# Third phase of a fused attention and expert-layer kernel worked in the order of the slots, with rows gathered once and scattered to the output

## The chip, the cores and the metric

One core of a Trainium2 chip runs the whole kernel. The metric is the device time of one execution in microseconds; the time of a kernel is the median of several executions. Engines are named as in the profile: PE (TensorE, with PEld for its weight loads), DVE (VectorE), ACT (ScalarE), POOL (GpSimd), SP (SyncE, which here only issues DMAs).

## The reference

The input x has 8 x 1024 rows (L = 8, N = 1024; 8192 tokens in all) of D = 256 numbers in float32. Two blocks follow each other, each with a residual and a layer norm:

```
x = LN0(x + A(x))       # A: 16 heads of 64 channels, attention among
                        # the 64 channels' scalars of each token, causal
x = LN0(x + F(x))       # LN0: layer norm without gain and offset
F(x):
  y1 = LN(x + MHA(x); ln1_g, ln1_b)   # 4 heads of 64, attention over L = 8
  gates = softmax(y1 @ wg); idx = argmax(gates)           # 8 experts
  loc  = rank of the token among those with its idx;  keep = loc < 1024
  slot = idx * 1024 + loc                                 # where keep
  disp[slot] = y1
  h = disp[e] @ w1[e] + b1[e];  o = h @ w2[e] + b2[e]     # no nonlinearity
  m = gate * o[slot] where keep, else 0
  return LN(y1 + m; ln2_g, ln2_b)
```

So a token that is late for a full expert gets no expert output, and the slots of an expert with fewer than 1024 tokens stay empty. At the end stand two norms in a row: F's, with ln2_g and ln2_b, then the outer LN0 over x + F(x).

## The kernel before, in words

`fused_kernel` (L46) runs three phases, one after the other. Rows are handled in 64 tiles of 128 tokens (NT), token t*128 + p on partition p.

`phase_a` (L85) is the first block. Its last instruction for a tile is a product with the output weights on PE (L408); then `r` (L413), the statistics and two small POOL operations (`norm_scalars`, L63: `ve` at L70, `rs` at L72), the normed tile (L419), and a store to the DRAM tensor x1_d on SP's queue.

`phase_b` (L506) is the attention over L, with 8 groups of 128 positions n (8 tiles of 128 tokens each, one per l). Beside the attention of group j (`scores`, `weights`, `weighted`) pieces of other work are set into the order by hand in `fills(j)` (L793): the projections of group j+1, the output rows of group j-1, and a quarter each of expert j's weights. The output rows go in four pieces of two l each: `output` (L704: POOL adds the offset to x in `residual`, L699, PE multiplies, DVE adds to `r`, L717), `normal` (L720: two DVE rows, then two POOL operations with ln1_g and ln1_b, L727, and a store to y1_d on SP), `turn_y` (L730, transposition) and `logits` (L743, copied to `lg` at L755). `expert` (L765) multiplies w1 by w2 of an expert into w12, since nothing nonlinear lies between them, and collects b1*w2 + b2 in `acc` on DVE (L782); `expert_bias` (L788) sums that over partitions with a product of ones into `bias`. In every group SP also stores zeros into disp_d (L867).

`phase_c` (L891) follows in four steps, in an order written out by hand for PE, ACT, DVE and SP, while POOL is scheduled by the framework.

1. Gating over all 64 tiles at once (L940 to L954): softmax of `lg`, the largest as `gate`, the first expert that has it as `hot`. Slots: prefix products on PE (L959, L961), a scan along the tiles (L963), `loc` (L970), then `to` and `back`, the row numbers to write to and to read from (L972 to L988). Meanwhile y1 is loaded into SBUF as `ya` (L909).
2. 64 indexed DMAs (L994), issued by POOL, write the rows of `ya` to their slots in disp_d.
3. Experts: 16 loads of 512 slots (`load`, L1012), transposition (L1024), products with w12 (L1050), plus bias (L1057), store to moe_d (L1064); x1 is loaded again into `xa` (L1045) and ln2_b added (L1065).
4. Norms, 16 turns of four tiles in token order (`order`, L1169): `fetch` (64 indexed loads from moe_d on POOL, L1089), `gates` (a diagonal matrix from the gate on ACT, L1102), `mix` (PE adds moe times gate and `ya` by products, L1115 and L1118), `stats` (L1130 and L1131), `power` (POOL, L1142), `offset` (L1147), `normed` (ACT, L1154), `gain` (DVE, ln2_g, L1164), the same once more with `xa` for the second norm, and a store to `out`.

Of the kernel before, what the change touches and what calls it, by code (L numbers as in the profile page):

```python
# [39 lines left out]
CAP = L * N // E  # L41
EPS = 1e-5
# [3 lines left out]
def fused_kernel(ctx: ExitStack, tc: tile.TileContext, a: dict, out: bass.AP):  # L46
# [12 lines left out]
    y1_d = dram.tile([L * N, D], FP, name="y1_d")  # L59
    disp_d = dram.tile([2 * E * CAP, D], FP, name="disp_d")  # L60
    moe_d = dram.tile([E * CAP + 1, D], FP, name="moe_d")

# [15 lines left out]
    w12 = late.tile([P, DC, E, D], FP, name="w12")  # L78
    bias = late.tile([P, E, D], FP, name="bias")
    lg = late.tile([P, NT, E], FP, name="lg")  # L80
    phase_b(tc, a, ident, x1_d, y1_d, disp_d, w12, bias, lg, norm_scalars)
    phase_c(tc, a, ident, x1_d, y1_d, disp_d, moe_d, w12, bias, lg, norm_scalars, out)


# [421 lines left out]
def phase_b(tc, a, ident, x1_d, y1_d, disp_d, w12, bias, lg, norm_scalars):  # L506
# [8 lines left out]
    with (  # L515
# [15 lines left out]
        for n in ("in_b_v", "out_b", "ln1_g", "ln1_b"):  # L531
            rows[n] = wp.tile([P, D], FP, name=f"row_{n}")
            nc.scalar.dma_start(rows[n], a[n].partition_broadcast(P))
# [7 lines left out]
        acc = wp.tile([P, E, D], FP, name="acc")  # L541
        nc.gpsimd.memset(acc, 0.0)
        nc.sync.dma_start(acc[0:1].rearrange("p e d -> p (e d)"), a["b2"].rearrange("(o e) d -> o (e d)", o=1))
        ones = wp.tile([P, P], FP, name="ones")
        nc.gpsimd.memset(ones, 1.0)
# [10 lines left out]
        zeros = wp.tile([P, 1024], FP, name="zeros")  # L556
        nc.gpsimd.memset(zeros, 0.0)
# [3 lines left out]
        y1_v = y1_d.rearrange("(l j p) d -> j p l d", p=P, j=NJ)  # L561
# [158 lines left out]
        def normal(j, l0):  # L720
            r, sc = G["r", j, l0]
            y = kp.tile([P, 2, D], FP, name="y")
            G["y", j, l0] = y
            for l in range(2):
                nc.vector.tensor_scalar(y[:, l, :], r[:, l, :], sc[l][0], sc[l][1], ALU.subtract, ALU.mult)
            for n, op in (("ln1_g", ALU.mult), ("ln1_b", ALU.add)):
                nc.gpsimd.tensor_tensor(y, y, rows[n][:, None, :].to_broadcast([P, 2, D]), op)  # L727
            nc.sync.dma_start(y1_v[j][:, l0 : l0 + 2, :], y)
# [14 lines left out]
        def logits(j, l0):  # L743
# [11 lines left out]
            nc.vector.tensor_copy(lg.rearrange("p (l j) e -> p l j e", j=NJ)[:, l0 : l0 + 2, j, :], ps[:, : 2 * E].rearrange("p (l e) -> p l e", l=2))  # L755
# [32 lines left out]
        def expert_bias(e):  # L788
            ps = pf.tile([P, 512], FP, name="fill")
            nc.tensor.matmul(ps[:, :D], ones, acc[:, e, :], start=True, stop=True)  # L790
            nc.scalar.copy(bias[:, e, :], ps[:, :D])

        def fills(j):  # L793
# [15 lines left out]
            put(0, not N and O, expert_bias, prv)  # L809
# [3 lines left out]
            put(0, N and O, expert_bias, prv)  # L813
# [27 lines left out]
            put(3, O, logits, prv, 6)  # L841
            put(3, X, expert, j, 3)
            put(3, N, project_qk, nxt, 1, 1, 0)
            put(3, N, project_qk, nxt, 1, 1, 1)
# [3 lines left out]
        for j in range(-1, NJ + 1):  # L848
# [4 lines left out]
            for n in range(4):  # L853
# [10 lines left out]
                if live:  # L864
                    if n < 2:
                        z = (2 * j + n) * 512
                        nc.sync.dma_start(  # L867
                            disp_d[z : z + 512, :].rearrange("(p r) d -> p (r d)", p=P), zeros
                        )
# [21 lines left out]
def phase_c(tc, a, ident, x1_d, y1_d, disp_d, moe_d, w12, bias, lg, norm_scalars, out):  # L891
# [4 lines left out]
    SH = 4  # L896
    with (
        tc.tile_pool(name="cone", bufs=1) as op,
        tc.tile_pool(name="cwork", bufs=4) as kp,
        ExitStack() as stage,  # L900
        tc.manual_schedule(engines={ET.PE, ET.Activation, ET.DVE, ET.SP}),
    ):
        pp = stage.enter_context(tc.tile_pool(name="cp", bufs=3, space=PSUM))
# [31 lines left out]
        def over_experts(v):  # L935
            return v[:, :, None].to_broadcast(ALL)

# [292 lines left out]
```

## Time and profile before

| what | us |
|---|---|
| median of three runs (5261.21 to 5263.25) | 5261.26 |
| the profiled execution's own time | 5258.0 |
| its span on the core (clock granted on average 0.978) | 5256.2 |
| PE busy | 4961.1 |
| DVE / ACT / POOL busy | 3013.8 / 3359.9 / 3364.5 |
| last product of phase A ends | 4335.2 |
| last logits copied (L755) | 4888.53 |
| first / last indexed store (L994) begins | 4907.49 / 4987.44 |
| first indexed load (L1089) | 5078.03 |

The span begins with the first and ends with the last instruction of the profiled execution, 1.8 us less than that execution's time. The page gives the busy time of each engine, the same in 40 slices, the DMA queues, the chain of work that ended last, and the costliest groups of instructions. In a row of a group: line, engine, operation, names of output and inputs, shapes and how many of them; after the bar the busy time and the mean in ns of one; after the second bar the idle time of the engine ahead of them and what ended it. The timeline gives start and length of each instruction in us, and in brackets how long its engine had been idle and on what it waited.

### The profile page before, as it was taken

Reading aid. Unit: us, or ns where it says so; the run is one execution under the profiler, and the core shown is the slowest. Engines: PE = TensorE matmul, PEld = TensorE weight load, DVE = VectorE, ACT = ScalarE, POOL = GpSimd, SP = SyncE. Lnnn points to the kernel's source line nnn. Section 1 sums busy time; section 2 is a strip of 40 time slices with the busy share of each in tenths; the row PEclk is TensorE's granted clock in tenths of the full one; section 3 lists DMA queues with packets and bytes.
Section 4 is the critical chain, followed back from the end, with each engine's and each line's share of the span. In section 5 each row is a group of like instructions: output and inputs, shape, how many; then the busy total and the mean of one; then the engine's idle time right before and its main releaser. Section 6 shows DMA issues by size and latency. Waiting matters only on the chain. (4 is left out here: it accounts for less than half of the span.)

```text
span 5256.2 us, 190381 instructions
## 1 busy us (share of the span) xinstructions
PE 4961.1 (94%) x80084; PEld 3377.1 (64%) x80084; DVE 3013.8 (57%) x5908; ACT 3359.9 (64%) x4114; POOL 3364.5 (64%) x6939
## 2 busy tenths in 40 slices
PE   8999999999999999999999999999999988997177
PEld 4666666666666666666666666666666655666066
DVE  5666666566665666666666656666656643555145
ACT  5777777777777777777777777777777763443025
POOL 5766776766767677666767766676777661333625
PEclk9999999999999999999999999999999998999599
DMA  2222222222222222222222222222222212221463
GB/s 75 47 48 48 48 48 48 48 47 47 48 48 49 48 49 47 47 48 48 48 47 49 48 47 48 48 49 48 49 48 46 48 40 88 90 93 57 143 218 98
DMA packets 603408, 313.53 MB, mean 60 GB/s; under 512 B 388146, under 2 KB 562355, under 8 KB 602547
## 3 DMA queue, kind: packets, MB, share of 16 engines
q1 hardware_dynamic: 396116, 147.14, 12.3%
q0 software_dynamic: 202752, 151.40, 9.7%
q8 instruction: 626, 10.26, 0.8%
q10 hardware_dynamic: 3680, 2.83, 0.2%
q14 instruction: 234, 1.92, 0.1%
HBM read 82.76 MB, written 50.33 MB: 25 GB/s over the span
## 5 line engine op out<-in xcount | busy, mean ns | idle before, releaser
L324 ACT ACTIVATE e<-pair 128x1024 f32<-128x1024 f32 x3072 | 2977.5, 1021 | 1236.3 <-PE pair L308 1236.3
L368 POOL DMA_DIRECT2D nd<-S x4096 | 1951.1, 484 | 612.2 <-DVE S L358 419.8
L308 PE MATMUL pair<-R,L 32*128 32x128 f32 (+1 forms) x32768 | 1606.3, 322 | 3.5 <-POOL event L279 3.5
L358 DVE COPY S<-sum 128x512 f32<-128x512 f32 x1024 | 707.2, 691 | 1469.4 <-PE sum L347 1159.3
L308 PEld LDWEIGHTS pair<-R,L 32*128 32x128 f32 x32768 | 1271.9, 186 | 49.7 <-POOL event L279 4.1
L338 PE MATMUL sum<-e,V 128*32 128x256 f32 x16384 | 1285.8, 385 | 4.9 <-DVE S L358 4.9
L265 POOL DMA_DIRECT2D R<-qm x2048 | 973.4, 483 | 73.5 <-issue 40.2
L347 PE MATMUL sum<-e,V 128*32 128x128 f32 x16384 | 823.7, 273 | 0.0
L347 PEld LDWEIGHTS sum<-e,V 128*32 128x32 f32 x16384 | 533.1, 110 | 352.8 <-issue 1.8
L338 PEld LDWEIGHTS sum<-e,V 128*32 128x32 f32 x16384 | 406.5, 109 | 236.8 <-DVE qm L232 41.8
L296 PE MATMUL pair<-late,sel 32*128 32x256 bf16 (+1 forms) x6144 | 499.4, 313 | 9.6 <-ACT e L324 9.6
L219 DVE COPY V<-vT 32x128 f32<-32x128 f32 x2048 | 456.8, 223 | 28.1
L377 DVE RECIPROCAL att<-nd 128x256 f32<-128x256 f32 x256 | 447.4, 1748 | 8.3 <-DMA nd<-S 4.4
L296 PEld LDWEIGHTS <-sel 32*128 32x128 bf16 x6144 | 155.5, 91 | 460.5 <-issue 445.1
L279 POOL MEMSET event<- 1x1 f32 x256 | 22.7, 89 | 615.4 <-DMA R<-qm 418.7
L188 PE MATMUL ps<-wk,xT 128*128 128x512 f32 x512 | 255.7, 622 | 11.8 <-DMA wk<-in_Wk 11.0
L199 PEld LDWEIGHTS ps<-xT,wv 128*128 128x128 f32 x2048 | 238.2, 191 | 44.4 <-issue 41.8
L199 PE MATMUL ps<-xT,wv 128*128 128x128 f32 x2048 | 262.6, 281 | 1.6 <-DVE qm L232 0.8
L231 PE MATMUL ps<-wq,xT 128*128 128x512 f32 x512 | 255.7, 622 | 5.4 <-DVE k L189 5.4
L408 PE MATMUL ps<-wo,attT 128*128 128x256 f32 x1024 | 257.9, 395 | 0.7 <-ACT attT L391 0.7
L70 POOL TENSOR_SCALAR ve<-mv 128x1 f32<-128x1 f32 x128 | 38.2, 299 | 320.6 <-DVE mv L68 319.1
L408 PEld LDWEIGHTS ps<-wo,attT 128*128 128x128 f32 x1024 | 186.2, 191 | 63.6 <-issue 41.8
(169 smaller groups left out, 3949.7 us busy)
## 6 DMA issues: line engine op xcount, KB each, us to landing
R<-qm POOLq DMA_DIRECT2D x2048, 32.0 KB
nd<-S POOLq DMA_DIRECT2D x4096, 16.0 KB
L<-k SPq DMA_DIRECT2D x4088, 8.0 KB
xT<-in_xT SPq DMA_DIRECT2D x64, 128.0 KB
xr<-in_x SPq DMA_DIRECT2D x64, 128.0 KB
x_d<-x1o SPq DMA_DIRECT2D x64, 128.0 KB
x<-x_d SPq DMA_DIRECT2D x8, 1024.0 KB
disp_d<-zeros SPq DMA_DIRECT2D x16, 512.0 KB
```

Of the source, the lines that this page charges most:

```text
L199: nc.tensor.matmul(ps[:, i * P : (i + 1) * P], w["v"][:, c, ch * P : (ch + 1) * P], xT_of[t][:, c, :], start=c == 0, stop=c == DC - 1,)
L219: nc.vector.tensor_copy(V[32 * aa : 32 * aa + 32, qd % 2, :, qd // 2, :, aa, 0:4], src[32 * qd : 32 * qd + 32, :, ww, :, aa, :],)
L265: moved.append((None, nc.gpsimd.dma_start(R[:, b, s, b, :], q[:, b, s, cols])))
L296: nc.tensor.matmul(bank[u].rearrange("p (n i) -> p n i", i=n)[:, :, 0:32], sel[pr].rearrange("p a j -> p (a j)"), late[pr, None, :].to_bro ...
L308: one = nc.tensor.matmul(bank[u][:, x * 4 * n : (x + 1) * 4 * n].rearrange("p (b i) -> p b i", i=n), Lt[pr, 2 * (h0 + h) + jb].rearrange(" ...
L324: nc.scalar.activation(e, pair[i], AF.Exp)
L338: nc.tensor.matmul(dst[32 * u : 32 * u + 32], Vs[ww][:, 0, h0 + h, u, :], e0[u // 2][:, u % 2, x * 256 : (x + 1) * 256].rearrange("p (b i) ...
L347: nc.tensor.matmul(dst[32 * u : 32 * u + 32, :, 32:], Vs[ww][:, 1, h0 + h, u, :], e1[u // 2][:, u % 2, h * 128 : (h + 1) * 128].rearrange( ...
L358: nc.vector.tensor_copy(S[:, :, 2 * which : 2 * which + 2, :].rearrange("p b h i -> p h b i"), ps.rearrange("p (h b i) -> p h b i", h=2, b=4),
L368: nc.gpsimd.dma_start(tok[:, b, s, h0 * C1 : (h0 + G) * C1], Sx[:, 4 if s else b, b, :])
L377: nc.vector.reciprocal(att[:, cols], nd[:, 1, cols])
L408: nc.tensor.matmul(ps[:, :D], attT[:, c, :], wo[:, c, :], start=c == 0, stop=c == HID // P - 1)
```

## The change

The three DRAM tensors y1_d, disp_d and moe_d give way to one, `rows_d`, with a row of 513 numbers (2052 bytes) for each token: y1, x1 + ln2_b and the gate. Phase B writes it: `normal` has a third POOL operation and stores rows of twice the length, and softmax, gate and choice of the expert are made for each group in `exps` and `choice`, which stand in the last part of `fills`. `expert_bias` and the stores of zeros are gone. The constants of phase C are made ahead of phase B (`constants`), `acc`, w12, `hot` and `red` live on into phase C, and ln2_g is loaded on ACT's queue ahead of phase B's weights.

In phase C every token gets a slot of its own, the late ones in the free slots of the experts that are not full (with `valid` to set their gate to 0). The token of each slot is then found by products of one-hot matrices: a slot number is split into `high` and `low` (low is the partition), and the sum over tokens of (low one-hot) x (high one-hot times the token's number) puts each token's number at its slot. With these numbers as indices, 16 turns of four tiles of slots run in one pipeline: gather four times 128 rows, transpose, multiply with w12 (the offset enters the same PSUM sum by a product of ones with `acc`), gate and residual, statistics, norm, gain and x1, statistics, norm, and 128 rows at a time are scattered to their tokens in `out`. The reciprocal root now is ACT's Sqrt with one Newton step and reciprocals on DVE (`roots`, `scales`). In the compiled order POOL has all the constants and the memset of `acc` ahead of the `ve` and `rs` of phase A's last tile; before, the memset of `acc` stood ahead of `ve`, and the memset of `ones` between `ve` and `rs`.

```diff
 # fused_kernel
-    y1_d = dram.tile([L * N, D], FP, name="y1_d")
-    disp_d = dram.tile([2 * E * CAP, D], FP, name="disp_d")
-    moe_d = dram.tile([E * CAP + 1, D], FP, name="moe_d")
+    rows_d = dram.tile([L * N, RW], FP, name="rows_d")          # RW = 2 * D + 1
...
+    constants(nc, late, keep)
+    nc.scalar.dma_start(keep["gain"], a["ln2_g"].partition_broadcast(P))
+    phase_b(tc, a, ident, x1_d, rows_d, keep, norm_scalars)
+    phase_c(tc, ident, rows_d, keep, out)
+def constants(nc, late, keep):
...
+    nc.gpsimd.memset(new("ones", [P, P]), 1.0)
+    make_upper_triangular(nc, new("before", [P, P]), val=1.0, diag=False)
+    rank = new("rank", [P, E])
+    for e in range(E):
+        nc.gpsimd.memset(rank[:, e : e + 1], float(E - e))
+    carry = new("carry", [P, E, NT])
+    nc.gpsimd.memset(carry, 1.0)
+    nc.gpsimd.memset(carry[:, :, 0:1], 0.0)
+    count("first", [P, E], [[CAP, E]], 0, 0)                    # count: iota on POOL
+    count("place", [P, NT], [[P, NT]], 0, 1)
+    count("column", [P, P], [[1, P]], 0, 0)
+    nc.gpsimd.memset(new("quarter", [P, 1]), 0.25 * EPS)
 # phase_b, normal(j, l0)
-            y = kp.tile([P, 2, D], FP, name="y")
+            yx = kp.tile([P, 2, 2 * D], FP, name="yx")
+            y = yx[:, :, :D]
...
+            nc.gpsimd.tensor_tensor(
+                yx[:, :, D:], G["x", j][:, l0 : l0 + 2, :], rows["ln2_b"][:, None, :].to_broadcast(both), ALU.add
+            )
-            nc.sync.dma_start(y1_v[j][:, l0 : l0 + 2, :], y)
+            nc.sync.dma_start(rows_v[j][:, l0 : l0 + 2, : 2 * D], yx)
 # phase_b, new
+        def exps(j):
...
+            nc.vector.tensor_reduce(top, lg, AX.X, ALU.max)
+            nc.vector.tensor_tensor(lg, lg, over_experts(top), ALU.subtract)
+            nc.scalar.activation(lg, lg, AF.Exp)
+        def choice(j):
...
+            nc.vector.tensor_reduce(total, lg, AX.X, ALU.add)
+            nc.vector.reciprocal(total, total)
+            nc.vector.tensor_tensor(lg, lg, over_experts(total), ALU.mult)
+            gate = kp.tile([P, L, 1], FP, name="gate")
+            nc.vector.tensor_reduce(gate[:, :, 0], lg, AX.X, ALU.max)
+            nc.sync.dma_start(rows_v[j][:, :, 2 * D :], gate, allow_slow_non_contiguous=True)
...
+            nc.vector.tensor_tensor(hot_v[:, j], rank, over_experts(red_v[:, j]), ALU.is_equal)
 # phase_b, fills(j)
-            put(0, not N and O, expert_bias, prv)
-            put(0, N and O, expert_bias, prv)
             put(3, O, logits, prv, 6)
+            put(3, O, exps, prv)
             put(3, X, expert, j, 3)
             put(3, N, project_qk, nxt, 1, 1, 0)
+            put(3, O, choice, prv)
             put(3, N, project_qk, nxt, 1, 1, 1)
 # phase_b, loop
-                        nc.sync.dma_start(
-                            disp_d[z : z + 512, :].rearrange("(p r) d -> p (r d)", p=P), zeros
-                        )
 # phase_c: after loc, made as before (tt: nc.vector.tensor_tensor), some 25 DVE operations, as
+        nc.vector.tensor_scalar(over, loc, float(CAP), None, ALU.is_ge)
+        nc.tensor.matmul(p_over[:, :NT], keep["before"], over, start=True, stop=True)
+        nc.tensor.matmul(p_over[:, NT : 2 * NT], keep["ones"], over, start=True, stop=True)
...
+        tt(steps, other[:, :, None].to_broadcast(ALL), skip[:, None, :].to_broadcast(ALL), ALU.is_ge)
+        tt(steps, steps, jump[:, None, :].to_broadcast(ALL), ALU.mult)
+        nc.vector.tensor_reduce(total, steps, AX.X, ALU.add)
...
+        nc.vector.scalar_tensor_tensor(low, high, -float(P), slot, ALU.mult, ALU.add)
+        K = 8
+        for k in range(NT // K):
+            ts = slice(K * k, K * k + K)
+            is_low = np_.tile([P, K, P], FP, name="is_low")
+            tt(
+                is_low,
+                low[:, ts, None].to_broadcast([P, K, P]),
+                column[:, None, :].to_broadcast([P, K, P]),
+                ALU.is_equal,
+            )
+            is_high = np_.tile([P, K, NT], FP, name="is_high")
+            tt(
+                is_high,
+                high[:, ts, None].to_broadcast([P, K, NT]),
+                column[:, None, :NT].to_broadcast([P, K, NT]),
+                ALU.is_equal,
+            )
+            nc.gpsimd.tensor_tensor(is_high, is_high, place[:, ts, None].to_broadcast([P, K, NT]), ALU.mult)
+            for i in range(K):
+                t = K * k + i
+                nc.tensor.matmul(
+                    p_tok[:, :NT], is_low[:, i, :], is_high[:, i, :], start=t == 0, stop=t == NT - 1
+                )
+        nc.vector.tensor_copy(token, p_tok[:, :NT])
...
+        def gather(q, i):
...
+            nc.gpsimd.indirect_dma_start(
+                out=st["g", q][:, i, :], out_offset=None, in_=rows_d,
+                in_offset=bass.IndirectOffsetOnAxis(ap=token[:, t : t + 1], axis=0),
+            )
+        def turned(q, pair):            # four transpositions on PE, nc.scalar.copy(xT, pt)
+        def product(q, pair):           # ones x acc[e] (128x512), then four products with w12
+        def spread(q, k, i, row):       # bn_stats, bn_aggr on DVE, for turn q + 1 + k
+        def blend(q, pair):
...
+                tt(st["gate", q], g[:, :, 2 * D], valid[:, Q * q : Q * q + Q], ALU.mult)
...
+                nc.vector.scalar_tensor_tensor(
+                    z[:, i, :], pr[:, (i % 2) * D : (i % 2 + 1) * D], st["gate", q][:, i : i + 1],
+                    g[:, i, :D], ALU.mult, ALU.add,
+                )
+                spread(q, 0, i, z[:, i, :])
+        def roots(turn):
...
+                nc.scalar.activation(h, mv[:, :, :, 1], AF.Sqrt, bias=keep["quarter"], scale=0.25)
+        def scales(turn):
...
+                nc.vector.reciprocal(rs, h)
+                nc.vector.scalar_tensor_tensor(ve, mv[:, :, :, 1], EPS, rs, ALU.add, ALU.mult)
+                nc.vector.scalar_tensor_tensor(ve, ve, 0.25, h, ALU.mult, ALU.add)
+                nc.vector.reciprocal(rs, ve)
+                nc.vector.scalar_tensor_tensor(nm, mv[:, :, :, 0], -1.0, rs, ALU.mult, ALU.mult)
+        def normed(k, q):               # four ACT rows, Identity with bias nm and scale rs
+        def join(q):
...
+            tt(n, n, keep["gain"][:, None, :].to_broadcast([P, Q, D]), ALU.mult)
+            tt(n, n, st["g", q][:, :, D : 2 * D], ALU.add)
+            for i in range(Q):
+                spread(q, 1, i, n[:, i, :])
+        def scatter(q, i):
...
+            if scattered:
+                nc.gpsimd.memset(gap, 0.0)
+            one = nc.gpsimd.indirect_dma_start(
+                out=out, out_offset=bass.IndirectOffsetOnAxis(ap=token[:, t : t + 1], axis=0),
+                in_=st["o", q][:, i, :], in_offset=None,
+            )
+        order = [                       # (step, its tile group's distance to the turn, ...)
+            (gather, -2, 0), (gather, -2, 1), (gather, -2, 2),
+            (roots, None),
+            (turned, -1, 0), (turned, -1, 1), (product, -1, 0), (product, -1, 1),
+            (blend, 0, 0), (scales, None), (normed, 1, 0), (blend, 0, 1), (normed, 2, 1),
+            (join, 1),
+            (scatter, 2, 0), (gather, -2, 3), (scatter, 2, 1), (scatter, 2, 2), (scatter, 2, 3),
+        ]
```

## The prediction

> **What bounds the kernel now.** I read the page first: PE busy 94% of the span, and in the row of 40 slices 8 and 9 nearly throughout, then a hole in the last three. The change touches little of phase A, so I cut the span at its own marks (end of phase A's last output product, end of phase B's steady work, last logits, first indexed store, first expert transposition, first indexed load) and asked for busy time by stretch. Columns: window, length, busy time of each engine, granted PE clock, DMA share, GB/s.
>
> ```profile
> core 0: us, PE busy (x) PEld busy (x) DVE busy (x) ACT busy (x) POOL busy (x), PEclk, DMA share, GB/s
> 0.00:4335.30 4335.30, 4289.04 (x76288) 2864.18 (x76288) 2599.95 (x4943) 3053.32 (x3201) 3013.76 (x6548) 1.00 0.21 48
> 4335.30:4840.00 504.70, 446.01 (x2771) 327.59 (x2772) 254.52 (x521) 201.43 (x671) 164.56 (x202) 0.96 0.27 85
> 4840.00:4888.50 48.50, 26.03 (x126) 21.18 (x125) 12.74 (x33) 6.79 (x17) 20.07 (x27) 0.71 0.07 22
> 4888.50:4907.50 19.00, 3.75 (x4) 1.18 (x4) 13.22 (x25) 0.63 (x1) 2.30 (x18) 0.59 0.94 300
> 4907.50:4993.80 86.30, 0.02 (x1) 0.02 (x1) 0.58 (x4) 0.00 (x0) 61.70 (x64) 0.50 0.40 141
> 4993.80:5077.10 83.30, 72.93 (x384) 61.44 (x384) 39.15 (x48) 21.11 (x40) 0.00 (x0) 0.98 0.88 293
> 5077.10:5256.20 179.10, 123.37 (x512) 101.49 (x512) 93.64 (x336) 76.65 (x184) 102.13 (x82) 0.89 0.30 94
> ```
>
> Phases A and B belong to PE. Everything after the last logits (4888.5) is 367.7 us in four stretches that do not overlap: gating and slots 19.0, indexed stores 86.3, experts 83.3, norms 179.1. In the stores only POOL works; in the experts POOL does nothing. The chain of waits says it again: an issue wait, then a load, then the experts.
>
> ```profile
> 4910.71 76.64 issue
> 4987.37 1.22 issue
> 4988.62 1.24 issue
> 4989.98 3.18 DMA xe<-disp_d
> ```
>
> The timeline gives the stores' period: 4908.96 to 4910.24, so 1.26 us each, 0.97 busy and 0.30 gap. The groups of the last stretch give the prices that I need.
>
> ```profile
> L1089 POOL DMA_INDIRECT g<-moe_d,back x64 | 62.3, 973 | 109.0 <-issue 107.3 <-PE ma L1118 1.7
> L1154 ACT ACTIVATE na<-ma,nma,scale 128x256 f32<-128x256 f32 x64 | 30.9, 563 | 74.1 <-DVE nmb L1147 45.2 <-DVE nma L1147 23.6 <-DVE mva L1131 5.3
> L1130 DVE BATCH_NORM_STATS2 s<-ma 128x6 f32<-128x256 f32 x64 | 26.1, 407 | 44.4 <-PE ma L1118 22.6 <-remote 11.7 <-PE ma L1115 10.1
> L1164 DVE TENSOR_TENSOR na<-na,row_ln_g 128x1024 f32<-128x1024 f32 x16 | 19.5, 1219 | 2.0 <-ACT na L1154 2.0
> ```
>
> **The sum, in order of time,** against the profiled span of 5256.2 (5258.0 executed; the median is 3.3 above that).
>
> *Up to the last logits.* (a) Between A and B the constants (memsets, triangle, eight rank columns, carry, iotas) now stand on POOL ahead of `acc`'s memset and of phase A's last `ve` and `rs` (L70, L72). From their rows in the old phase C they cost about 2.45 us. Behind them wait the last x1 tile's DVE step (L419), its store on SP, phase B's first load of x and, on it, PE (first L575 at 4349.83). The store left 1.7 us after its data (4338.99 to 4340.68), so about +1; bounds −1 to +3. (b) In a group of phase B, `normal` issues a third POOL op of 1.27 (the row of L727), 4 per group. POOL is only 33% busy there (164.56 of 504.70), but its queue is in order: `residual` (L699) for rows 4 stands behind two of the new ops, 2.54 later. In the group that I followed, `r` (L717), which waits for it, ended at 4633.37 and would end at 4635.9, and PE begins the next logits, for which that PSUM buffer must be free, at 4635.15. I take +0.9 for that, −0.43 for the lost bias product, and a little DVE and ACT for `exps` and `choice`: +0.5 in each of 8 groups, +4; bounds −4 to +14. (c) After the last group PE has little to do and two of the new ops lie on the path to the last rows: +2.5. The gate's 4-byte elements go out on SP ahead of the next expert load, which is needed many us later: nothing, and at most the few us that 1024 small pieces take at the last group, under the slot arithmetic. Sum +7.5: last logits at 4896.0.
>
> *Slots.* What is left of the gating is 8 tiles' worth of small ops, about 2.8 where the full-size one took 8.5 (4888.5 to 4897.0): 4898.8. The two prefix products and their wait as before, 4.1: 4902.9. Scan to `loc`, as before 4.4: 4907.3. New: three 128x512-sized ops (0.69, 0.69, 1.01) and some 22 dependent small ones at the 0.23 of L976 to L984: 7.5, ending at 4914.8 (bounds 6 to 9).
>
> *Token of each slot.* Eight rounds of DVE 128x1024 (1.22, L1164's size) and 128x512 (0.69), POOL 128x512 (1.27), PE 8 products. Here a rule has to be weighed against rows. A DVE op with two SBUF inputs alone, and beside POOL:
>
> ```profile
> 4501.90 0.97 DVE L782 SCALAR_TENSOR_TENSOR acc<-w,b,acc 128x256 f32<-128x256 f32 x2
> ...
> 4514.99 1.89 DVE L782 SCALAR_TENSOR_TENSOR acc<-w,b,acc 128x256 f32<-128x256 f32 x2
> 4515.21 1.38 POOL L727 TENSOR_TENSOR y<-y,row_ln_g 128x512 f32<-128x512 f32 x1 [0.58 <-issue]
> ```
>
> The pair took 0.92 longer although POOL's op cost only 0.11 more than its usual 1.27: they did not share, DVE stood still between its two. The Trainium skill (page "SBUF — State Buffer", section "SBUF: two separate sides") has the shared port pair as "an exclusive lock, not a bandwidth split", for the whole instruction. Row and rule exclude each other's overlap; without it a round is the longer of 1.91 and 1.27, with it the sum, 3.18 + 0.10 of handing over = 3.28. So 8 × 3.28 = 26.2 instead of 15.6. I take 26.2, the other as lower end. With the last products and the copy of `token`, 2.0: 4943.0.
>
> *Filling the pipeline.* Four indexed loads 5.0, landing 3.2 (an estimate: 2.8 behind the last issue in the old chain, for rows half as long), transposition, copy and product 3.5: first `blend` at 4954.7.
>
> *A turn of four tiles,* 16 of them:
> - DVE: gate 0.2; four rows of `blend` at 0.48 (half of L782's 0.97) + 0.61 with two statistics (0.535 apart in the timeline) and hand-over = 4.4; `scales`, five small dependent ops, 1.0; `join`, two 128x1024 ops, 2.5; its four statistics 2.1. Sum 10.2.
> - POOL: 4 loads and 4 stores at 1.26 = 10.1. The memset before a store fits into the 0.30 gap (a compute op beside it leaves 0.17 to 0.19).
> - ACT: two copies 1.2, eight rows of `normed` at 0.49 as pipelined, roots 0.2, about 6; PE under 6. Covered: each has 4 us to spare. ACT's table for roots is one extra load (1.28 at the start of this trace), once, under DVE's first turn.
> - A ring: a turn's last load is queued behind its first store, which waits for `normed`; its rows must be issued and land (3.5: 0.75 and the old 2.8), be transposed and copied (1.4) before the next turn's `normed` on ACT's queue. Store 1.26 + landing 3.5 + 1.4 + `normed` 4.1 = 10.3. No longer than the others.
>
> Three limits lie within 0.2 of each other, so what is added to POOL counts. A load issued under DVE's two-input op is held:
>
> ```profile
> 5105.39 0.97 POOL L1089 DMA_INDIRECT g<-moe_d,back  x1 [0.30 <-issue]
> ...
> 5106.10 1.23 DVE L1164 TENSOR_TENSOR na<-na,row_ln_g 128x1024 f32<-128x1024 f32 x1 [2.00 <-ACT na L1154]
> ...
> 5106.66 1.49 POOL L1089 DMA_INDIRECT g<-moe_d,back  x1 [0.30 <-issue]
> ```
>
> It took 1.49 in place of 0.97: 0.5 late, ending 0.8 after DVE did; the load before, already begun, lost nothing and cost DVE nothing. [...] by that rule a store caught at the start of both `join` ops loses all 2.5 (turn 12.6); by the row about half an op, 0.6 to 0.9 a turn. I take the row: POOL 10.1 + 0.9 = 11.0 a turn; 16 × 11.0 = 176: 5130.7. Bounds 10.2 and 12.6.
>
> *End.* Turn 16 (scales, `normed`, `join`) 8.1, turn 17 (roots, scales, `normed`, four stores, landing) 9.4: 5148.2.
>
> So −108.0 against 5256.2. In short: of 367.7 us after the logits, 252.2 remain (2.8 + 4.1 + 4.4 + 7.5 + 28.2 + 11.7 + 176 + 17.5), −115.5, and +7.5 ahead of them. What goes is the 86.3 in which POOL worked alone and the reloading of x1 and of the experts' rows through memory; what becomes the bound is DVE and POOL together in 16 turns. Median: 5261.26 − 108 = 5153.
>
> **Rivals.**
> - *The port costs the full 2.5 a turn.* For it: stores and `join` fall into the same half of the turn. Against it: loads begun before the lock run through. 16 × 1.6 = +25.6: 5179.
> - *No port conflict counts.* Turn 10.2 (−12.8), one-hot rounds 15.6 (−10.6): 5130. The L782 rows speak against the second half.
> - *POOL's third op in `normal` lies on PE's path in full.* 32 × 1.27 = 41 in place of 4: 5190. For it: PE waited for `y` (L727) and `r` (for L699) in the trace. Against it: POOL has over half of phase B free.
> - *Indexed transfers queue behind each other's landing,* and it ends slower. Each row is now 2052 bytes and not a multiple of a round length, and stores to `out` have a memset between them. If each of a turn's 8 waited until the one before had landed, 3.5 each, the turn is 28: 16 × 17 = +272, 5425. It turns to slower once the start-to-start time passes 2.2 us: 108 / 16 = 6.75 more a turn, 17.75 / 8. For it: no store to `out` by index exists in this trace. Against it: the 64 stores and 64 loads that do exist ran at 1.26 without waiting for landing.
>
> **How the numbers follow.** Chances: forecast 0.60, full port cost 0.20, no conflict 0.12, POOL in phase B 0.05, landing in series 0.03. Low end 5128: no conflict, with 2 for the constants. High end 5188: full port cost, with 9 of phase B's bound. A measurement of this kernel can tell 0.2% (10 us) from no change; of the cases only the last is slower, and a mixture of the dear ones could just reach no change: faster 0.96, same 0.01, slower 0.03.
>
> **What would show it.** Right: last logits about 7 later; eight one-hot rounds at 3.2 to 3.4 with DVE and POOL alternating; turns of 10.5 to 11.5 with POOL over 90% busy; some loads or stores at 1.5 to 2 us, all beginning under `join`. Wrong: turns near 10.2 with DVE full (no conflict), near 12.6 with stores behind both `join` ops, or a start-to-start time of loads above 1.4 outside them; one-hot rounds at 1.9; PE waiting more than 2 us more a group for `y` or `r`.

## The result, and the profile after

The changed kernel takes 5176.94 us in the median of four runs (5169.03 to 5183.43). The kernel before, run beside it, took 5261.24 (5259.65 to 5263.25). The ratio is 0.9839, 95% interval 0.9822 to 0.9856: faster by 1.6%, 84 us where 108 were forecast. The time lies in the predicted range and 24 above the predicted point. The profiled execution took 5169.03, the fastest of the four, with a span of 5167.3; stages below are compared within spans.

Experiments 1 to 4 ran on one chip, 5 to 8 on a second and 9 to 12 on a third, each time beside the kernel before. The same changed kernel stood at 0.9839 here and at 0.9926 on the third chip, so stages are compared from their own beginnings, and ratios only on one chip.

The span of after, cut at the same marks as that of before (same columns): end of phase A, end of phase B's steady work, last logits, first one-hot operation, last one, first `blend`, end of turn 15's `join`, end.

```profile
core 0: us, PE busy (x) PEld busy (x) DVE busy (x) ACT busy (x) POOL busy (x), PEclk, DMA share, GB/s
0.00:4332.30 4332.30, 4288.56 (x76288) 2863.52 (x76288) 2600.03 (x4943) 3053.11 (x3201) 3010.27 (x6547) 1.00 0.21 49
4332.30:4840.00 507.70, 433.28 (x2595) 315.41 (x2596) 250.02 (x549) 190.21 (x633) 180.09 (x226) 0.94 0.31 76
4840.00:4918.70 78.70, 49.80 (x286) 41.22 (x285) 32.21 (x76) 16.67 (x56) 44.32 (x51) 0.74 0.24 74
4918.70:4936.25 17.55, 4.59 (x8) 2.10 (x8) 12.54 (x41) 0.26 (x1) 0.00 (x0) 0.60 0.03 0
4936.25:4968.20 31.95, 27.57 (x128) 27.38 (x128) 16.82 (x18) 0.00 (x0) 10.07 (x8) 0.50 0.00 1
4968.20:4980.60 12.40, 6.75 (x19) 4.12 (x20) 0.20 (x1) 1.17 (x2) 9.55 (x10) 0.55 0.64 174
4980.60:5142.80 162.20, 116.98 (x431) 81.05 (x429) 147.63 (x432) 80.15 (x163) 113.46 (x165) 0.84 0.45 135
5142.80:5167.30 24.50, 0.00 (x0) 0.00 (x0) 6.28 (x20) 6.68 (x14) 9.77 (x17) 0.50 0.15 54
```

The 86.3 us in which POOL worked alone and the experts' own 83.3 are gone: in the long stretch DVE is busy 147.63 of 162.20, POOL 113.46, PE 116.98. Two rows speak against the forecast. In the one-hot stretch PE is busy 27.57 of 31.95 at a clock of 0.50, an engine whose price the sum had left out. And the last logits stand at 4918.7, where 4896.0 were predicted, with PE's clock down from 0.96 to 0.94 in phase B.

By stage:

| stage | predicted us | measured us | difference |
|---|---|---|---|
| last logits, at | 4896.0 | 4918.7 | +22.7 |
| rest of gating, prefix products, scan to `loc` | 11.3 | 10.9 | −0.4 |
| extra slot arithmetic | 7.5 | 6.6 | −0.9 |
| one-hot rounds to `token` | 28.2 | 31.7 | +3.5 |
| filling | 11.7 | 12.65 | +0.95 |
| 16 turns | 176 | 162.1 | −13.9 |
| turn 16 | 8.1 | 8.35 | +0.25 |
| turn 17 and end | 9.4 | 16.2 | +6.8 |
| span | 5148.2 | 5167.3 | +19 |

Two errors are large and opposite, so the good total is partly luck.

**Where phase B's time went.** Take the interval from the first row maximum (`mx`) to the copy of the last logits: 510.0 before, 541.1 after, 31.1 more. By `mx` to `mx`, four to a group, the middle groups took 60.8 to 62.4 before and 63.5 to 66.8 after, the last part-group 39.3 and 51.1. The seven intervals before the last part sum to +18.8, the last part to +11.8, the tail to +0.5.

The first `mx` comes 1.1 earlier, but the boundary between the phases isn't free. From phase A's last product to phase B's first product it took 14.6 before and 18.5 after; in the twelve experiments, where POOL has the same order there, it took 17.7 to 18.3. That is 3.0 to 3.8 more than in the one trace of before. First PE products of phase B, before and after:

```profile
4349.83 1.51 PE L575 MATMUL fill<-ident,x 128*128 128x128 f32 x6 [14.64 <-DMA x<-x_d]
```

```profile
4350.71 1.51 PE L607 MATMUL fill<-ident,x 128*128 128x128 f32 x6 [18.47 <-DMA x<-x_d]
```

In this profile two things hid it: phase A ended 2.9 earlier, and the way from the first product to `mx` was 2.0 shorter. Both differ as much among traces of the same code (phase A's end from 4331.2 to 4337.2, that way 26.7 or 28.4 to 28.7). Of the terms of phase B's sum only the tail, predicted at +2.5, was not too small.

PE's waits of after in phase B's steady part (4424 to 4865): engine, tile, line, what it waited for, us in total, times, longest.

```profile
PE fill L773 <- POOL yx L761: 29.7, 9, 6.6
PE pw L841 <- DMA w<-in_w: 11.4, 6, 6.0
```

Before, the same two were 24.9 (longest 6.6) and 1.8 (longest 1.5). PE now waits 9.6 more for the expert's weights. The longest of these waits is in the last group; the timeline (start, length) shows what stood ahead of the load on SP's queue.

```profile
4797.73 0.88 SPq L829 DMA_DIRECT2D w<-in_w  x1
4808.31 0.37 SPq L817 DMA_DIRECT2D rows_d<-gate  x1
4808.79 0.52 SPq L827 DMA_DIRECT2D w<-in_w1T  x1
4809.40 0.41 SPq L829 DMA_DIRECT2D w<-in_w  x1
...
4817.92 0.77 PE L841 MATMUL pw<-w,w 128*128 128x256 f32 x1 [6.03 <-DMA w<-in_w]
```

The weights were issued at 4809.40 and used at 4817.92. Two things made them late. First, from 4798.6 to 4808.31 SP issued nothing: the gate's store is the next in its order and waits for the gate, and the load waits behind it. So the load leaves 2.5 ahead of the group's first `mx` (4811.9). In before the same load left 13.8 ahead of it (4794.3):

```profile
4780.47 0.40 SPq L762 DMA_DIRECT2D w<-in_w  x1
```

Second, the gate's 4 KB go ahead of it through the DMA engines, and they are 1024 pieces. The DMA view of the stretch 4547.9 to 4556, where the same store stands ahead of the same loads in an earlier group, counts them:

```profile
DMA packets 1574, 0.54 MB, mean 67 GB/s; under 512 B 1066, under 2 KB 1573, under 8 KB 1573
```

In that stretch of before there were 2 packets. By their own records the 4-byte packets took only 7.8 us of engine time, some 7 ns each. But the 507 packets of 1 KB behind them, which are the loads, took 97.8 us; at their median of 46 ns each they would have taken 23. So the pieces cost the loads, by this estimate, 75 us of engine time, or 4.7 us of all 16 engines.

The waits cost twice. Stretches of 4 us around one wait for `yx` (3.06 us long there, 2.38 for `y` in before: experiments 1, 2 and 7 show that the missing bias product makes the difference, and not POOL's third operation), columns as above:

```profile
4566.00:4570.00 4.00, 1.52 (x18) 1.17 (x14) 3.93 (x9) 0.81 (x6) 3.48 (x5) 0.97 0.00 0
4570.00:4574.00 4.00, 3.42 (x10) 2.93 (x11) 0.67 (x1) 3.60 (x15) 3.92 (x4) 0.50 0.33 113
4574.00:4578.00 4.00, 4.00 (x22) 2.59 (x21) 1.12 (x2) 0.58 (x1) 2.82 (x3) 0.68 0.95 259
```

After a stretch with 1.52 us of work PE is granted half its clock, here for 6.8 us, in the other five middle groups for 3.4 us at a time. Each 3.4 us cost 1.7 where PE has work. In before this happened in one of six middle groups, in after in all six.

**A turn.** Timeline of after, around a `join`: DVE's two 128x1024 operations, the store issued under the first, and the load behind it.

```profile
5065.39 1.22 DVE L971 TENSOR_TENSOR n<-n,gain 128x1024 f32<-128x1024 f32 x1
...
5066.36 1.13 POOL L1204 DMA_INDIRECT out<-o,token  x1 [0.22 <-ACT o L1186]
5066.65 1.23 DVE L971 TENSOR_TENSOR n<-n,g 128x1024 f32<-128x1024 f32 x1
...
5067.80 0.96 POOL L1083 DMA_INDIRECT g<-rows_d,token  x1 [0.30 <-issue]
```

The store takes 1.13 in place of 0.97: it is issued 0.97 into the first operation, and the second, which begins 0.29 after it, doesn't hold it. The other turns agree: with 0.25 of the operation left a store takes 1.12, with 0.49 left 1.33, and the load of before, which had 0.66 left, took 1.49. An issue is held for 0.10 to 0.14 less than what is left, and no longer. So POOL lost some 0.15 a turn, not 0.9. From 5050 to 5082 none of DVE's rows has idle time ahead of it: the steady turn of 10.3 to 10.4 is DVE's sum.

### The profile page after: what moved, and what is told of

Same layout as the page of the kernel before. It is cut to its first block, busy times and chain, and to the rows that moved or that the text cites. A ratio compares the mean times of both kernels' runs of the same rounds, so it can differ in the third digit from the quotient of the medians.

```text
span 5167.3 us, 189788 instructions
## 1 busy us (share of the span) xinstructions
PE 4927.5 (95%) x79752; PEld 3334.8 (65%) x79752; DVE 3065.7 (59%) x6079; ACT 3348.2 (65%) x4067; POOL 3377.5 (65%) x7022
```

## The experiments

Three hypotheses for phase B: (1) PE lost filler work (the bias products, 128x256) that used to bridge its wait for `y`, so that the clock drops; (2) POOL's third operation and the longer store delay the loads behind them on SP; (3) the gate's small pieces do. And one for the one-hot rounds: the shared port, or PE. B is the interval from the first `mx` to the last logits (before 510.0, after 541.1).

**1. The filler put back.** A product of the same size, and its copy, at the old places.

```diff
+        def filler(e):
+            ps = pf.tile([P, 512], FP, name="fill")
+            nc.tensor.matmul(ps[:, :D], keep["ones"], acc[:, e, :], start=True, stop=True)
+            unused = kp.tile([P, D], FP, name="unused")
+            nc.scalar.copy(unused, ps[:, :D])
...
+            put(0, not N and O, filler, prv)
+            put(0, N and O, filler, prv)
```

> The product of ones with acc (128x256) and its ACT copy are put back into part 0 of each group of phase B, where expert_bias stood before; their result is not used. Clock theory: without that product PE reaches the transposition of y 0.7 us earlier and waits 3.06 instead of 2.4 us in each of 7 groups, and the longer wait lets the granted PE clock drop to about half for one period of some 3.4 us, 1.7 us lost each. Then the waits go back to about 2.4, the clock in those stretches to 1.00, and the kernel gains 6 to 12 us: 5165 to 5171. Theory that POOL's third operation or the stores are the whole cost: the product adds its own 0.4 us in 8 groups, 5180.

Measured: 5168.54 (5167.17 to 5173.87), ratio 0.9836 (0.9822 to 0.9849), B 538.1. The waits for `yx` went back to 2.33 to 2.38, as they should by (1), but waits for `r` of 1.7 came in three groups, and the clock still dropped about once a group. Three us are no more than B differs between runs of the same phase B (541.1 to 547.0 over the four kernels that have it unedited). The time lies in the range that was expected if (1) held, but on this chip the kernel before was 4.2 faster too, and the ratio is that of after. The filler is not the main cause.

**2. x1's half made by itself and stored ahead of the next group's loads.** `normal` has two POOL operations again.

```diff
-            nc.sync.dma_start(rows_v[j][:, l0 : l0 + 2, : 2 * D], yx)
+            nc.sync.dma_start(rows_v[j][:, l0 : l0 + 2, :D], y)
+        def row_x(j):                   # four POOL additions into xx, last part of the group
+        def send_x(j):
+            nc.sync.dma_start(rows_v[j][:, :, D : 2 * D], G["xx", j])
...
+            put(0, O, send_x, prv)
+            put(3, X, row_x, j)
```

> x + ln2_b is no longer the third POOL operation of normal; it is made for a whole group in that group's part 3, when POOL is idle, and stored with one DMA in the next group. POOL theory: the wait of logits for r goes, SP's stores and the expert loads behind them come earlier and PE's waits for expert weights at the end of a group (0.5 to 2.2 us) go, and the tail of phase B gets 2.5 us shorter: 5163 to 5169. Clock theory: the waits of 3.06 us for y and the clock drops stay, only the tail gains: 5174.

Measured: 5216.91 (5211.36 to 5221.26), ratio 0.9919 (0.9905 to 0.9932), B 588.0: 47 worse, against what was expected of it. PE's waits from 4424 to 4870 say why:

```profile
PE pw L851 <- DMA w<-in_w: 39.2, 7, 7.2
```

The 1 MB store now stands ahead of each group's expert loads, and they come late in every group. It removed the suspected cost and made a larger one of the same kind: what counts is what SP has in front of a load that is needed soon.

**3. The gate stored a group later, in the third part.**

```diff
-            nc.sync.dma_start(rows_v[j][:, :, 2 * D :], gate, allow_slow_non_contiguous=True)
+            G["gate", j] = gate         # the last group's is stored at once
...
+            put(2, prv >= 1, send_gate, prv - 1)
```

> The store of the gate's 4-byte elements moves from the end of a group to part 2 of the next one, behind that part's expert load. Theory of the small pieces: the 6.0 us wait for expert weights in the last group goes, with the clock drop behind it: 5167 to 5171. Otherwise nothing: 5175 to 5179.

Measured: 5200.09 (5194.76 to 5204.19), ratio 0.9891 (0.9876 to 0.9906), B 569.6: 28 worse, against what was expected. The wait of 6.0 did go, and the last part-group took 43.1 in place of 51.1. But at the new place, too, expert loads are right behind the pieces: PE's waits for `pw` rose to 32.0 in 7 places, 5.4 to 6.0 in the four groups to which they were moved, and these groups to 71 to 72. The gate is long ready there, so SP isn't held for it; the pieces, and a load of x between them and the weights, are enough for 5 to 6 us of lateness each time. At the gate's place in after most groups have slack for it, the last one doesn't.

**4. All three edits.** Experiments 1, 2 and 3 in one kernel.

> All three edits of phase B together. If the three causes add up: 5145 to 5155, last logits 20 to 26 us earlier than in the changed kernel. If one of them hides another: above 5160.

Measured: 5231.27 (5226.25 to 5236.58), ratio 0.9949 (0.9935 to 0.9962), B 605.1. The single effects, −3.0, +46.9 and +28.5, sum to +72.4; together they gave +64.0, nearly additive: two different transfers delay the loads at two different places.

Experiments 5 to 8 took the loads themselves, and turned to the one-hot rounds.

**5. Each quarter of an expert's weights loaded one quarter ahead.**

```diff
+                load_expert(0, 0)
...
-                    load_expert(j, n)
+                    if 4 * j + n + 1 < 4 * NJ:
+                        load_expert(*divmod(4 * j + n + 1, 4))
```

> Every quarter of an expert's weights is loaded one part of a group earlier, before the stores that SP would otherwise issue ahead of it; nothing else changes. Theory of late loads: PE's waits for expert weights (0.5 to 2.2 us in most groups, 6.0 us in the last) go, with the clock drops behind them; groups fall from 64 to about 62.5 us: 5158 to 5166. Theory that POOL's third operation delays r and y and the clock does the rest: only the last group gains: 5170 to 5174.

Measured: 5194.73 (5188.79 to 5200.88), ratio 0.9876 (0.9860 to 0.9893), B 525.9, 15.2 less than after; the first `mx` comes 5.9 later, so the last logits gain 9.4. The 5.9 are not the price of the extra pair of loads at phase B's start: experiment 6 has the same pair and its first `mx` at 4377.1, and kernels without an edit in phase B differ as much (4377.4 to 4384.0). PE's waits from 4424 to 4860:

```profile
PE fill L773 <- POOL yx L761: 29.8, 9, 6.6
PE fill L785 <- DVE r L749: 3.4, 2, 1.7
```

The wait for the weights is gone, and the one for `yx` as it was. The late loads were half of B's 31.1. The whole time, though, is worse than after's first figure: from the first `blend` to the end it took 227.5 where after took 186.7, and nothing was changed there (experiment 9).

**6. Loads ahead, with the edits of 1 and 2.**

> Loads one part ahead as in e5, x + ln2_b made in part 3 as in e2, and the unused product of ones with acc back as in e1. If e2 and e3 were slow only because the separate store stood in front of expert loads, its waits for weights (4 to 7 us a group) are gone now, and the groups come back to the 60.8 us of the kernel before: 5144 to 5152. If POOL's operations next to each other or the DMA traffic itself are the cost: groups stay above 63 us, above 5165.

Measured: 5191.56 (5190.00 to 5194.46), ratio 0.9876 (0.9859 to 0.9892), B 520.6. The edit that cost 47 when the loads were late costs nothing when they are early, and B is 20.5 below after's. No wait for weights or `r` is left in the groups, and B lies 10.6 above before. The clock drops in four of six groups, three more than in before: 3 × 1.7 = 5.1. The two groups without a drop take 62.3, still 1.5 more than the usual 60.8. PE's waits show where it is, before (4424 to 4840) and in this run (4424 to 4850):

```profile
PE fill L684 <- ACT sT L674: 11.2, 7, 1.7
```

```profile
PE fill L716 <- ACT sT L706: 19.5, 13, 1.7
```

The six more stand late in the six groups, 1.4 each, where neither before nor after waits for `sT`: 8.4. Together 13.5, and the six groups lie 13.1 above before's; the rest of B is 2.5 shorter. In that place POOL makes its four additions, and DVE's scaling of `mx` (128x8), beside the last of them, takes 0.68 in place of 0.17. What else makes this wait was not followed.

**7. x1 copied by ACT in place of POOL's third operation.** It leaves out the addition of ln2_b.

```diff
-            nc.gpsimd.tensor_tensor(
-                yx[:, :, D:], G["x", j][:, l0 : l0 + 2, :], rows["ln2_b"][:, None, :].to_broadcast(both), ALU.add
-            )
+            nc.scalar.copy(yx[:, :, D:], G["x", j][:, l0 : l0 + 2, :])
```

> POOL's third operation in normal is replaced by an ACT copy of x; ln2_b is left out of the sum. DMAs are unchanged. POOL theory: the wait of logits for r goes, stores go out 1.3 to 2.5 us earlier and the waits for expert weights at the end of most groups with them, and the end of phase B is 2.5 us shorter: 5155 to 5165. If the rows of twice the length and the gate's pieces are the cost: 5172 to 5178, and the waits for weights stay.

Measured: 5196.02 (5190.82 to 5198.22), ratio 0.9879 (0.9863 to 0.9896), B 527.0, 14.1 less. Without the third POOL operation the stores leave SP sooner and all waits for weights but the last group's (5.8) are below 1.2. No wait for `r` is left either, while the one for `yx` stays at 3.0 to 3.15. The sum is like experiment 5's, but it falls elsewhere: 6.4 in the six middle groups (5.5 there), 3.1 in the last part-group (6.9) and 5.9 in the tail (3.9).

**8. The one-hot's multiplication on DVE.** The port between DVE and POOL is then no matter.

```diff
-            nc.gpsimd.tensor_tensor(is_high, is_high, place[:, ts, None].to_broadcast([P, K, NT]), ALU.mult)
+            nc.vector.tensor_tensor(is_high, is_high, place[:, ts, None].to_broadcast([P, K, NT]), ALU.mult)
```

> The product of the high one-hot with the token numbers moves from POOL to DVE, so that POOL takes no part in the eight rounds. Port theory (DVE and POOL exclude each other): a round falls from 3.41 to the 2.6 us of three DVE operations, 5 to 7 us less in all. PE theory (128 short products with a weight load each at half clock, 0.21 us each): a round stays at 3.41, and only the first rounds and the last hand-over gain, 0 to 2 us.

Measured: 5210.93 (5206.99 to 5212.18), ratio 0.9908 (0.9892 to 0.9925); one-hot stage 30.4, 1.3 less than 31.7. The first rounds take DVE's 2.47, then DVE waits for PE:

```profile
4952.62 1.23 DVE L971 TENSOR_TENSOR is_low<-low,column 128x1024 f32<-128x1024 f32 x1 [0.74 <-PE pr L1059]
```

The period is then 3.41, as in after. Not the port sets it, but PE.

**9. After, without an edit,** because the turns of experiments 5 to 8 had all become longer.

> The changed kernel itself once more, unedited, beside e10 to e12. In the four kernels of e5 to e8 ACT sat some 6 us longer than its inputs ask for in every second of the 16 turns, about 41 us in all, and in e1 to e4 and the changed kernel never. If the place (chip or moment) decides, then the four of this call all have it or all lack it: with it this kernel takes 5205 to 5222, without it 5168 to 5184. If the edits of e5 to e8 decide, this one lacks it whatever the others do.

Measured: 5218.73 (5210.54 to 5222.12), ratio 0.9926 (0.9914 to 0.9938). B 541.3 and one-hot 31.7 as on the first chip, but 226.7 from the first `blend` to the end. So the 40 us belong to the chip or the moment and not to the edits, and the right base for experiments 10 to 12 is 5218.73. The timeline of this run shows what a long turn (16.0 to 16.5, every second one) waits for:

```profile
5055.72 0.65 PE L1097 MATMUL ps<-ident,g 128*128 128x128 f32 x2 [1.64 <-DMA g<-rows_d,token]
...
5060.07 0.95 POOL L1083 DMA_INDIRECT g<-rows_d,token  x1 [0.30 <-issue]
...
5063.35 1.07 ACT L1101 COPY xT<-ps 128x512 f32<-128x512 f32 x2 [8.33 <-remote]
```

ACT's copy needs the transpositions, the last of which ended well before by their rows; it begins some 6 us later than they ask, with a releaser that the profile calls "remote". It resumes 3.3 after the last gather was issued, about when its rows are there. ACT itself may not be the one that is late: in the trace the semaphore with which PE tells of its transpositions is raised at 5063.33 and 5063.40, while their rows end at 5052.48 and 5056.37. In after's turns it is always raised within 0.1 of such an end. PE's ends are modelled, so either its signal is late or its work is.

**10. The fourth gather moved up,** straight behind the third: if ACT waits for rows that come late, they should come earlier.

```diff
+            (gather, -2, 3),
             (roots, None),
...
-            (scatter, 2, 0), (gather, -2, 3), (scatter, 2, 1), (scatter, 2, 2), (scatter, 2, 3),
+            (scatter, 2, 0), (scatter, 2, 1), (scatter, 2, 2), (scatter, 2, 3),
```

> The fourth gather of a turn is issued with the first three, ahead of the turn's first scatter, so that its rows land some 3 us earlier and PE's wait for them (1.7 us in each turn) goes. Theory that DVE is full in a turn: the turn stays at 10.3 to 10.4 us, the time within 3 us of the control. Ring theory (scatter, gather, landing, copy, normed): the turn falls below 10.2. If ACT's extra 6 us come from rows that land late, they are gone here, also where the control has them: about 40 us less than such a control.

Measured: 5213.03 (5207.37 to 5215.47), ratio 0.9914 (0.9901 to 0.9927). The long turns went from 16.4 to 15.9 and not to 10.4, so late rows are not the reason. The short ones stayed at 10.4 although the ring of store, gather and transposition was cut: DVE bounds the turn, as its rows say.

**11. Experiments 6 and 10 together.**

> The edits of e6 (expert weights one part ahead, x + ln2_b in part 3, the unused product) with the gathers of e10. Phase B 20 us shorter than in the control, as in e6; with the order of e10 5148 to 5158 where ACT has no extra idle time.

Measured: 5188.07 (5183.80 to 5191.64), ratio 0.9871 (0.9856 to 0.9885), B 519.9. It is faster than both kernels here: 30.7 below the unedited one on the same chip. Most of that is phase B. On the first chip it was not run.

**12. Experiment 8 with eight 128x512 products ahead of the one-hot,** to raise PE's clock.

```diff
+        for _ in range(8):
+            p_warm = pq.tile([P, 512], FP, name="pr")
+            nc.tensor.matmul(p_warm, keep["ones"], flat, start=True, stop=True)
```

> As e8 (the token numbers multiplied in on DVE), and PE gets 8 products of 128x512 while DVE works out the slots; their result is not used. Clock theory: PE enters the one-hot rounds at full clock and its 16 short products of a round take 1.7 us, not 3.4; if the clock lasts through the rounds DVE is the bound at 2.6 a round, 6 us less than e8's 41.3 us from the scan to the token copy. If the clock falls again within a few us because the products are short and mostly weight loads, 0 to 3 us less.

Measured: 5208.64 (5203.26 to 5218.88), ratio 0.9904 (0.9889 to 0.9920); one-hot stage 26.6, and all of DVE's rounds 2.47 long. Two stretches of it (columns as above):

```profile
4955.00:4961.00 6.00, 4.90 (x41) 4.49 (x39) 5.89 (x8) 0.00 (x0) 0.00 (x0) 1.00 0.01 3
4961.00:4967.00 6.00, 5.85 (x28) 5.85 (x28) 5.93 (x8) 0.00 (x0) 0.00 (x0) 0.50 0.00 0
```

At full clock (from 4947.3 to 4961.0) PE does 41 matmul records, of which a product has two, in 4.90 us of 6, and DVE is the bound. Then the clock falls back to 0.50, though PE was hardly idle, and PE lags again. It hid the lag for a while, and so the stage gained 5.1 against after's.

## Why the prediction was right, and where it failed

**Right: the sign, and what is removed.** The 86.3 in which POOL worked alone are gone and the third phase is bound by DVE and POOL together. DVE's sum for a turn, 10.2, measured 10.3 to 10.4. Gating, prefix products, slot arithmetic, filling and turn 16 each came within 1 us.

**Failed: (b) "+0.5 in each of 8 groups, +4; bounds −4 to +14", and the gate's pieces, "needed many us later: nothing".** Measured: +18.8 in seven groups and +11.8 in the last part. The wait for `r`, on which the +0.9 rested, is real: 1.7, in none to four of the six middle groups of the five traces with this phase B, and gone without the third operation (experiment 7). The larger part lies elsewhere. The prediction followed POOL's third operation through POOL's queue to `r`, but not on through SP's: the store of `yx` waits for it, and the expert loads are queued behind that store. In the group that was followed the store is issued 2.97 before the next `mx` in before and 1.75 before it in after (4536.37; 4538.12), and the loads behind it land 7 to 9 us after their issue. Experiments 5 and 7 each give back 14 to 15 by cutting this chain at either end; both together were not run. The gate's store is the second part: a wait of 6.0 in the last group, and 5.4 to 6.0 where experiment 3 put it. "Nothing" was argued from the time at which the data was needed, without the price of 1024 pieces ahead of it, and without the 9.7 us for which SP's order holds the load back until the gate is there. Of the rest, 10.6 in experiment 6, 5.1 is PE's clock, and the waits for `sT` make up more than the other half. In after the clock drops around the waits of 3.06; but putting the filler back shortened them and did not cure it (experiment 1), and one wait of 3.00 in experiment 7 passed without a drop. So why it drops stays open.

The Trainium skill (page "TensorE: Matmul & The Clock Gate", section "Part 1: The HAM clock gate (the "warmup" mystery)") has the clock halved after an idle window of about 3.4 us and restored after as long a busy one. The length of the slow stretches agrees: 3.4 or a multiple of it. The rest doesn't: waits of 1.7 to 3.1 us stood ahead of the drops in the middle groups, and in the one-hot stage PE was busy 27.57 of 31.95 us by the profile without being given its clock. The measurement decides; in this case busy time in the profile doesn't tell what the gate grants.

**Failed, and hidden in the total: (a) "about +1; bounds −1 to +3".** Measured: +3.8, in the experiments +3.0 to +3.7. The part that was summed was right: x1's last data came 4.9 after phase A's last product in place of 3.8, so 1.1 later. But their store left SP 3.5 after them in place of 1.7, and the load of x 4.2 behind the store in place of 3.2. Why was not tried.

**Failed: the one-hot's cause; its number was near by chance.** "With it the sum, 3.28" took the port as the bound. Rounds with the lock are seen only at the start; timeline of after, an early and a late round:

```profile
4938.01 1.22 DVE L971 TENSOR_TENSOR is_low<-low,column 128x1024 f32<-128x1024 f32 x1
4938.26 1.86 POOL L1056 TENSOR_TENSOR is_high<-is_high,place 128x512 f32<-128x512 f32 x1 [22.34 <-DVE is_high L971]
4939.14 1.53 DVE L971 TENSOR_TENSOR is_high<-high,column 128x512 f32<-128x512 f32 x1
...
4950.72 1.23 DVE L971 TENSOR_TENSOR is_low<-low,column 128x1024 f32<-128x1024 f32 x1 [1.58 <-PE pr L1059]
...
4954.13 1.23 DVE L971 TENSOR_TENSOR is_low<-low,column 128x1024 f32<-128x1024 f32 x1 [1.59 <-PE pr L1059]
```

The early one is the lock at work: POOL's operation, 1.04 alone, takes 1.86, and DVE's second, 0.68 alone, 1.53. They take turns, and the next round begins at 4940.59, after 2.58. The three one after the other would take 2.78 (1.74 from DVE's first to its next round where nothing held it, and 1.04), so little overlaps. But the sum's 3.28 had POOL at 1.27: with the lock alone eight rounds would take about 21, not 26.2, by these rows. The late one lasts 3.41 and DVE waits 1.59 of it for PE: eight short products with their weight loads at half clock. The sum had "PE 8 products" and no price for them. Experiment 8, without the lock, gains 1.3; experiment 12, with PE at full clock for part of the time, 5.1.

**Failed: the port in the turns, "half an op, 0.6 to 0.9 a turn".** Measured some 0.15, as the store falls late into the first operation. The row from which 0.5 was taken had its issue near the middle of an operation; the price depends on where the issue falls, and the prediction had not placed it. (Its 1.26 a store was read from rows that are 1.28 apart; over all 64 the mean is 1.27, so this adds only 0.1 a turn.) So POOL needs about 10.2 and DVE's 10.35 decides; and since one of the first 16 turns has no `join`, they sum to 162.1. This is the rival "no port conflict" in the turns.

**Failed: the end, "9.4".** Scales, stores and landing were priced well: the last packet for `out` ends 8.1 after turn 16. But the span ends 8.0 after this packet, with one fetch of 8 KB of instructions in the DMA records and nothing else. In before, too, 4.5 lay between the last such packet and the end; the sum had forgotten it. All thirteen traces with the new third phase have the 8.0. Why it is longer now wasn't tried.

The measured median lies 2 from the rival "the port costs the full 2.5", 5179, but its turn of 12.6 did not occur. The time fits it, the profile refutes it.

## What to carry to other kernels

Follow an operation that is added ahead of a store beyond its own engine: on the queue that issues the store, look for the load that stands next, and ask how soon its data is used. A queue that issues in order also holds the load back as long as the store ahead waits for its own data, and a store of many small pieces is priced by the piece. Give every engine in a round a price, at the clock that the trace grants it in such a stage, before calling one hidden. And when a total fits, check the stages: here 23 and −14 stood behind it.

## What the runs showed of the hardware that was not expected

- 1024 stores of 4 bytes, 4 KB in all, cost the loads behind them about 5 us of all 16 DMA engines (an estimate): the loads' packets of 1 KB took 193 ns in the mean, at a median of 46.
- PE kept a clock of 0.50 through 32 us of dense short products, and lost the full clock after 13.7 us of it (experiment 12).
- On two of the three chips, in all profiled runs there, ACT began about 6 us late in every second turn of the pipeline, some 40 us in all (222 to 228 in place of 187 from the first `blend`); on the third, and in the profile of after, never. The gathered rows are not late (experiment 10), but PE's signal comes late, by the trace. The cause is open.
- The Trainium skill (page "SBUF — State Buffer", section "SBUF: two separate sides") calls the port an exclusive lock; the early rounds come near it, 2.58 where three operations in sequence would take 2.78. But an issue of an indexed store is held only by the operation that it falls into, 0.15 here, and not by the one that follows, which begins 0.03 after it.
